# Scaling by 1 / std in the dealt output stages: from VectorE to GpSimd

## The chip, the core and the metric

The kernel runs on one core of a Trainium2 chip. The metric is the device time of one launch in microseconds (us). Everything is float32. Of the core's engines four compute here: TensorE (PE in the profile, with its weight loads as PEld), VectorE (DVE), ScalarE (ACT) and GpSimd (POOL). SyncE (SP) issues most of the DMAs. Each engine works through its own instruction stream in program order and waits for the others by semaphores.

## The reference

Two layers follow one another on x of shape (8, 64, 64, 192): `x = x + L(gn(x))`. Each L is a selective-scan block with 384 inner channels and 16 states; the first has 2 scan directions, the second 4. Cut to what matters here:

```python
xz = in_proj(gn(x)); xx, z = split(xz)
xc = silu(depthwise_conv3x3(xx))
for each direction:                    # 2 in the first layer, 4 in the second
    delta, Bs, Cs = projections of xc in that direction's order
    h = exp(delta * A) * h + (delta * xc) * B    # over 4096 positions
    y += sum over states of h * C                # plus xc * D
y = (y - mean(y)) * rsqrt(var(y) + 1e-5) * w + b # over the 384 channels
y = y * act(z)                                   # gelu, then silu
out = x + y @ out_proj
```

The change concerns the last four lines, the output stage, and in it the factor `rsqrt(var(y) + 1e-5)`, here called 1 / std.

## The kernel before, in words

**Tiling.** The 4096 positions of an image are cut into 8 chunks of T = 512. Channels lie on the 128 partitions, in DT = 3 channel tiles. A layer first runs a front part (`front`: projection and convolution for all 8 images) and then `scans`, which the change touches. There the work is a list of steps: for each image, for each direction, for each of 8 chunks. That makes 128 steps in the first layer and 256 in the second.

**Slots.** A step has NSL = 24 slots: 8 pairs of states times 3 channel tiles. In each slot DVE scans two states (`scan`, L736, two `tensor_tensor_scan` of 512) and POOL multiplies the result by C (`hc`, L737, 128x1024). Before that, PE must have put the scan's input into PSUM (`inject`, `hb`, L695, 16 matmuls), two slots ahead with two buffers, and ACT must have made the decay factors (`decay`, `da`, L712, two activations), four slots ahead with five buffers. After it, PE sums the products of a group of three slots into `py` (`reduce`, `py`, matmuls recorded at L152), 24 matmuls for each of the group's two states; the two are emitted at slots 5 and 5 after the group's first in the first layer, at 5 and 6 in the second. `h` has two buffers, `hc` and the C rows `cr` three each, all by groups of three slots. So the first layer has 3072 slots and the second 6144.

**Order.** The order on each engine is written out by hand. Everything that is not one of the four regular operations is entered with `at(step, slot, function)` at a slot given in a table (`L0_SLOTS`, `L1_SLOTS`), and the loop at the end emits it:

```python
                if 0 <= g < N * NSL:
                    scan(i, s)
                for f, a in sorted(todo.pop(g, []), key=lambda fa: rank_of.get(fa[0], 1.5)):
                    f(*a)
                if 0 <= g + 2 < N * NSL:
                    inject(g + 2)
                if 0 <= g + 4 < N * NSL:
                    decay(g + 4)
```

So in a slot each engine gets the scan's part first, then the entered functions, then the injection for two slots on and the decay for four slots on. Slot numbers above 23 run on into the following steps. "Slot 72" of the second layer is thus slot 0 of the third step after the one in which an output stage begins.

**Dealt output stages.** While image b + 1 is scanned, the 8 output stages of image b are dealt out: one every 2 steps (48 slots) in the first layer, one every 4 steps (96 slots) in the second. With 7 images and 2 layers these are 112 dealt stages. The output stages of the last image (8 in each layer, tables `L0_LAST` and `L1_LAST`) have their own slots and are called "own stages" below; their scaling stays where it was. A dealt stage runs on tile `yc` of 128 x 3 x 512:

- mean by matmuls, kept through the one-buffer tile `sm` (L871), and subtracted on DVE (`f_center`, L878); the squares likewise, ending in `pm` in PSUM
- `f_rstd`: Ln (L885) and Exp with scale -0.5 (L886) on ACT, both in PSUM
- `f_scale`: one DVE multiplication of all three tiles by 1 / std out of PSUM (L889)
- `f_affine`: weight and bias, ACT, one instruction for each channel tile (L897)
- `f_times`: product with the gate, POOL, one for each channel tile (L906)
- `f_out`: the output projection, PE, 3 matmul pairs for each of two output halves (`po`, L912), and `f_add`, DVE (L921)

The small PSUM results (`pd`, `pt`, `pb`, `pq`, `pz`, `ps`, `pm`, `po`) share one buffer, tag "m": the next can be written only when the one before it has been read.

Near a dealt stage's scaling in the second layer, the slot tables also place the preparation of the next step: `x_proj` (`pd`, L560) at slots 73, 73 and 75, its copy `x_dbl` (L570, ACT) at 76, `dt_proj` (`pt`, L608) at 77, 80 and 82, and `keep_y` at slot 77: the ACT copy (L785) of the finished step's `py` out of PSUM. `py` has one buffer, so the first `reduce` of the running step, also emitted at slot 77, waits for that copy.

Of the kernel before, what the change touches and what calls it, by code (L numbers as in the profile page):

```python
# [8 lines left out]
F32 = mybir.dt.float32  # L9
AF = mybir.ActivationFunctionType  # L10
# [5 lines left out]
P = 128  # L16
# [8 lines left out]
DT = 3  # L25
NS = 16
T = 512
NCH = L // T
RB = T // W
Q = 32  # L30
# [38 lines left out]
    "f_center": 24,  # L69
    "f_square": 24,  # L70
    "f_rstd": 33,
    "f_scale": 33,
    "f_act": 34,
    "f_affine": (36, 35, 34),
    "f_times": (38, 39, 36),
    "f_out": ((42, 42, 42), (44, 46, 46)),
    "f_add": (43, 47),
}

L0_LAST = {  # L80
# [35 lines left out]
    "f_center": 48,  # L116
    "f_square": 48,
    "f_rstd": 72,
    "f_scale": 72,
    "f_act": 59,  # L120
    "f_affine": (72, 76, 72),
    "f_times": (76, 79, 72),
    "f_out": ((83, 84, 84), (89, 91, 94)),
    "f_add": (85, 95),
}
# [377 lines left out]
def scans(tc, name, x_src, x_dst, xcd, xcd_col, xtd, xdd, t, dirs, rank, row_b, gate, slots, last, consts, dram):  # L503
# [5 lines left out]
    nc = tc.nc  # L509
# [27 lines left out]
    with tc.tile_pool(name=f"{name}_s1", bufs=1) as s1, tc.tile_pool(  # L537
        name=f"{name}_s2", bufs=2
    ) as s2, tc.tile_pool(name=f"{name}_psy", bufs=1, space=PSUM) as psy, tc.tile_pool(
        name=f"{name}_psh", bufs=2, space=PSUM  # L540
# [4 lines left out]
        def at(i, s, f, *a):  # L545
            todo.setdefault(i * NSL + s, []).append((f, a))
# [248 lines left out]
        fin = {}  # L795
# [71 lines left out]
                )  # L867

        def f_keep_sum():
            fin["sm"] = s1.tile([DT * Q, T], F32, name="sm")  # L870
            nc.scalar.copy(fin["sm"], fin["ps"][: DT * Q])  # L871

        def f_all(key):
# [7 lines left out]
            fin["sq"] = s1.tile([P, DT, T], F32, name="y" if end else "xn_sq")  # L881
            nc.scalar.activation(fin["sq"], fin["y"], AF.Square)

        def f_rstd():
            nc.scalar.activation(fin["pv"], fin["pv"], AF.Ln, bias=eps_ln)  # L885
            nc.scalar.activation(fin["pv"], fin["pv"], AF.Exp, scale=-0.5)  # L886

        def f_scale():
            nc.vector.tensor_mul(  # L889
# [40 lines left out]
        def thrice(i, s, f, *a):  # L930
            for p, q in enumerate(s):
                at(i, q, f, *a, p)

        for i in range(N):
# [22 lines left out]
            b, k, cols, rev, ci, c = steps[i]  # L957
# [9 lines left out]
        e = 0  # L967
        for b in range(B - 1):
            for c in range(NCH):
                e = max(e + K, (b + 1) * K * NCH - NCH + c + 1)  # L970
                at(e, 0, f_load_x, b, c)
                at(e, 6, f_load, b, c)
                at(e, slots["f_norm"], f_norm, b, c)
                for dt in range(DT):
                    thrice(e, slots["f_gate"][dt], f_gate, dt)
                    at(e, slots["f_keep"][dt], f_keep, dt)
                for w, (src, key) in enumerate((("y", "pm"), ("sq", "pv"))):
                    at(e, slots["f_sum"][w], f_sum, src)
                    at(e, slots["f_keep_sum"][w], f_keep_sum)
                    at(e, slots["f_all"][w], f_all, key)  # L980
                for f in f_center, f_square, f_rstd, f_scale, f_act:
                    at(e, slots[f.__name__], f)
                for dt in range(DT):
                    at(e, slots["f_affine"][dt], f_affine, dt)
                    at(e, slots["f_times"][dt], f_times, dt)
                for u in range(CT):
                    thrice(e, slots["f_out"][u], f_out, u)
                    at(e, slots["f_add"][u], f_add, u)
                at(e, slots["f_add"][1], f_store, b, c)
        for c in range(NCH):  # L990
            b, e, own = B - 1, N - NCH + c + 1, last
            if c == NCH - 1:

                own, l = dict(last), last["load"]
                at(N - 1, 20, f_load_last, b, c)
                own["f_norm"], own["f_act"] = l, l + 4
                own["f_gate"] = [(l + d, l + d) for d in range(DT)]
                own["f_keep"] = [l + d + 1 for d in range(DT)]
                own["f_mean"] = [[l + 5] * DT, [l + 7] * DT]
                own["f_center"], own["f_square"], own["f_rstd"], own["f_scale"] = l + 6, l + 6, l + 8, l + 9  # L1000
                own["f_affine"], own["f_times"] = [l + 10, l + 10, l + 11], [l + 11, l + 11, l + 12]
                own["f_out"], own["f_add"] = [[l + 12, l + 12, l + 13], [l + 15] * DT], [l + 14, l + 16]
                at(e, l, f_load, b, c)
            else:
                at(e, own["load"], f_load_x, b, c)
                at(e, own["load"], f_load, b, c)
            at(e, own["f_norm"], f_norm, b, c)
            for dt in range(DT):
                thrice(e, own["f_gate"][dt], f_gate, dt)
                at(e, own["f_keep"][dt], f_keep, dt)  # L1010
            for w, (src, key) in enumerate((("y", "pm"), ("sq", "pv"))):
                thrice(e, own["f_mean"][w], f_mean, src, key)
            for f in f_center, f_square, f_rstd, f_scale, f_act:
                at(e, own[f.__name__], f, *((c == NCH - 1,) if f is f_square else ()))
            for dt in range(DT):
                at(e, own["f_affine"][dt], f_affine, dt)
                at(e, own["f_times"][dt], f_times, dt)
            for u in range(CT):
                thrice(e, own["f_out"][u], f_out, u)
                at(e, own["f_add"][u], f_add, u)  # L1020
            at(e, max(own["f_add"]), f_store, b, c)
# [29 lines left out]
def vss_layer(tc, name, x_src, x_dst, w, dirs, rank, row_b, gate, slots, last, consts, dram):  # L1051

    with ExitStack() as ctx:
        xcd, xcd_col, xtd, xdd, *dram = dram
        if any(cols for cols, rev in dirs):
            xdd = None
        else:
            xcd_col = None
        t = load_weights(tc, ctx, name, w, len(dirs), rank, row_b + 2 * NS, consts[1])
        clear = dram[-1] if xcd_col is None else ()  # L1060
        front(tc, name, x_src, xcd, xcd_col, xtd, xdd, w["in_proj"][:, :D], t, clear, consts)
        scans(tc, name, x_src, x_dst, xcd, xcd_col, xtd, xdd, t, dirs, rank, row_b, gate, slots, last, consts, dram)
# [99 lines left out]
```

## Time and profile before

| What | Value |
|---|---|
| time, median of 3 runs | 26029.92 us (26021.06 to 26032.92) |
| profiled execution, its own time | 26028.44 us |
| span of that execution, first to last instruction | 26026.6 us |
| granted TensorE clock, mean | 0.988 |
| scans of the first layer | from 1025 to 9136 us, 3072 slots, 2.64 us each |
| scans of the second layer | from 10337 to 25982 us, 6144 slots, 2.55 us each |
| POOL busy / instructions | 22104.7 us / 9615 |
| L737 on POOL | x9216, mean 2370 ns |
| L878 on DVE, the subtraction of the mean | x128, mean 1730 ns |
| L885 and L886 on ACT, Ln and Exp | x128 each, mean 654 and 582 ns |

A "busy" share counts the time in which an engine has an instruction under way. Idle time in a row stands just before the instruction, with the engine and line that ended it. A timeline row merges instructions of one group that follow each other: start, duration of the whole row, engine, line, output and inputs, count. Instructions of one engine overlap by some hundredths of a microsecond, so the distance between two starts is a little shorter than the mean duration.

### The profile page before, as it was taken

The numbers are of one execution on the slowest core, as the hardware profiler recorded it, in microseconds if no ns is written. First come the engines' busy times: TensorE is split into PE (matmuls) and PEld (weight loads), VectorE is DVE, ScalarE is ACT, GpSimd is POOL, SyncE is SP. The second block draws the span as 40 slices with busy tenths as digits, with TensorE's granted clock in tenths as the row PEclk, the third lists the DMA queues.
The fourth block names the chain that finished last, engine by engine and source line by source line (L and its number), as shares of the span: only waits on it lengthen the run. The fifth ranks groups of instructions, "written<-read, shape, count | busy, mean of one in ns | idle before, by whom it ended". The sixth has DMA issues, their size and how long they took to land.

```text
span 26026.6 us, 785972 instructions
## 1 busy us (share of the span) xinstructions
PE 24190.1 (93%) x340032; PEld 13575.8 (52%) x340032; DVE 24270.1 (93%) x22142; ACT 17787.7 (68%) x28084; POOL 22104.7 (85%) x9615
## 2 busy tenths in 40 slices
PE   8999999999999877999999999999999999999999
PEld 4455555555555533555555555555555555555554
DVE  7899999999999855999999999999999999999998
ACT  4567777777777655666767767767767767767766
POOL 0399999999999701999999999999999999999997
PEclk9999999999999988999999999999999999999999
DMA  4566666666666556576576576576576576576574
GB/s 153 145 154 158 153 154 154 155 158 155 156 155 154 136 149 159 163 161 166 164 164 166 164 163 166 163 163 166 163 164 167 163 163 167 164 163 167 164 163 140
DMA packets 4225339, 4140.59 MB, mean 159 GB/s; under 512 B 2532524, under 2 KB 2732868, under 8 KB 4221892
## 3 DMA queue, kind: packets, MB, share of 16 engines
q1 hardware_dynamic: 3819760, 4032.72, 60.1%
q10 hardware_dynamic: 402132, 57.59, 1.3%
q8 instruction: 2692, 44.11, 0.7%
q14 instruction: 755, 6.18, 0.1%
HBM read 3443.63 MB, written 645.99 MB: 157 GB/s over the span
## 4 chain that ended last, share of the span: by engine, by line
PE 40%; DVE 38%; ACT 10%; issue 9%; ACTq 1%; DMA 1%; POOL 0%; SPq 0%; DVEq 0%; POOLq 0%
DVE h L736 33%; PE hb L695 17%; PE py L152 11%; ACT da L712 3%; PE pt L608 2%; PE pz L835 2%; PE pd L560 2%; PE po L912 2%; DVE tp L353 2%; DVE dut L658 1%; ACT delta L145 1%; ACT L145 1%; PE pc L152 1%; ACT L632 1%; ACTq L384 1%
## 5 line engine op out<-in xcount | busy, mean ns | idle before, releaser
L737 POOL TENSOR_TENSOR hc<-h,cr 128x1024 f32<-128x1024 f32 x9216 | 21639.8, 2370 | 3773.7 <-DMA xt_k<-xtd 2178.2
L736 DVE TENSOR_TENSOR_SCAN h<-da,st,hb 128x512 f32<-128x512 f32 x16128 | 19187.5, 1258 | 629.8 <-PE hb L695 560.6
L712 ACT ACTIVATE da<-delta,a_neg 128x512 f32<-128x512 f32 x18432 | 12142.9, 713 | 3225.2 <-DVE h L736 3218.7
L695 PEld LDWEIGHTS hb<-dg,dut 64*128 64x128 f32 x147456 | 9260.3, 186 | 7083.1 <-issue 5877.6
L695 PE MATMUL hb<-dg,dut 64*128 64x128 f32 x147456 | 10909.6, 287 | 908.9 <-DVE h L736 639.5
L152 PE MATMUL py<-hc,mask 32*32 32x512 f32 x147456 | 6882.8, 603 | 0.2
L152 PEld LDWEIGHTS py<-hc,mask 32*32 32x32 f32 x147456 | 1571.9, 103 | 2348.3 <-issue 1770.6
L736 DVE TENSOR_TENSOR_SCAN h<-da,hb 128x512 f32<-128x512 f32 x2304 | 2611.8, 1199 | 135.1 <-PE hb L695 122.4
L742 ACT COPY st<-h 128x6 f32<-128x6 f32 x2688 | 532.9, 198 | 1844.2 <-DVE h L736 1843.7
L353 DVE SCALAR_TENSOR_TENSOR tp<-pad,cw,tp 128x512 f32<-128x512 f32 x1344 | 991.0, 750 | 592.3 <-ACT tp L347 537.8
L608 PE MATMUL pt<-xdbl,w_dt 96*128 96x512 f32 (+1 forms) x2304 | 1302.9, 647 | 49.5 <-DVE yc L878 34.9
L650 PE MATMUL pq<-ident,delta 128*128 128x128 f32 x4608 | 760.4, 288 | 387.7 <-DVE dut L658 333.7
L622 ACT ACTIVATE delta<-pt,dtb 128x512 f32<-128x512 f32 x1152 | 783.9, 681 | 485.4 <-PE pt L608 485.3
L835 PE MATMUL pz<-xn_sq,w_in 96*128 96x512 f32 x1536 | 826.1, 637 | 38.0 <-ACT xn_sq L823 14.8
L658 DVE TENSOR_TENSOR dut<-pq,xt_k 128x512 f32<-128x512 f32 x1152 | 765.8, 665 | 88.2 <-PE pq L650 88.2
L560 PE MATMUL pd<-x_k,w_x 128*128 128x512 f32 x1536 | 798.3, 629 | 30.9 <-DVE yc L878 15.1
L912 PE MATMUL po<-yc,w_out 128*96 128x512 f32 x1536 | 787.4, 624 | 16.8 <-POOL yc L906 15.0
L650 PEld LDWEIGHTS pq<-ident,delta 128*128 128x128 f32 x4608 | 485.2, 141 | 586.9 <-DVE dut L658 472.7
L321 PE MATMUL pi<-x,w_x 128*128 128x512 f32 x768 | 427.0, 664 | 313.7 <-ACT x L301 124.1
L906 POOL TENSOR_TENSOR yc<-yc,g 128x512 f32<-128x512 f32 x384 | 491.0, 1281 | 126.4 <-ACT yc L897 123.6
L152 PE MATMUL pc<-pad,taps 32*32 32x512 f32 x13824 | 575.9, 592 | 12.2 <-ACT xo L368 12.2
L145 ACT ACTIVATE delta<-delta 128x1536 f32<-128x1536 f32 x384 | 570.5, 1486 | 4.3
(105 smaller groups left out, 9921.3 us busy)
## 6 DMA issues: line engine op xcount, KB each, us to landing
cr<-cscr SPq DMA_DIRECT2D x2048, 512.0 KB
dg<-dgd SPq DMA_DIRECT2D x1536, 512.0 KB
cr<-xdd SPq DMA_DIRECT2D x1024, 512.0 KB
xt_k<-xtd SPq DMA_DIRECT2D x768, 384.0 KB
xcd<-xo SPq DMA_DIRECT2D x128, 768.0 KB
xtd<-xv SPq DMA_DIRECT2D x128, 768.0 KB
y<-yrow SPq DMA_DIRECT2D x128, 768.0 KB
yc<-yrow SPq DMA_DIRECT2D x128, 768.0 KB
```

Source lines behind the costliest of these rows:

```text
L145: nc.scalar.activation(out, in_, AF.Softplus)
L152: nc.tensor.matmul(out[j * Q : (j + 1) * Q, dt], w[i * Q : (i + 1) * Q], x[i * Q : (i + 1) * Q], start=first, stop=last, tile_position=(i ...
L353: nc.vector.scalar_tensor_tensor(tv, window(dt, c, s), cw[:, dt, s : s + 1], tv, ALU.mult, ALU.add)
L560: nc.tensor.matmul(live[i]["pd"][:R], w_x[:, dt, k, :], live[i]["x"][:, dt], start=(dt == 0), stop=(dt == DT - 1),)
L608: nc.tensor.matmul(pt, w_dt[:, k, dt * P : (dt + 1) * P], live[i]["xdbl"][:rank], start=True, stop=True,)
L650: nc.tensor.transpose(pq[:, g], live[i]["delta"][:, dt, g * P : (g + 1) * P], ident)
L695: nc.tensor.matmul(hv[:, r, q], live[i]["dut"][r * G : (r + 1) * G, dt, q], dg[r * G : (r + 1) * G, q, :, 2 * mm : 2 * mm + 2], start=True ...
L712: nc.scalar.activation(da[:, n].rearrange("p (r g j) -> p r g j", r=2, j=G), live[i]["delta"][:, dt].rearrange("p (g r j) -> p r g j", r=2 ...
L736: nc.vector.tensor_tensor_scan(o, a, v, init, ALU.mult, ALU.add)
L737: nc.gpsimd.tensor_mul(hc[:, dt], h[:, dt], live[i]["cr", m])
L835: nc.tensor.matmul(fin["pz"], w_in[:, u, dt * P : (dt + 1) * P], fin["xn"][:, u], start=(u == 0), stop=(u == CT - 1),)
L912: nc.tensor.matmul(fin["po"][:CP], w_out[:, dt, u * CP : (u + 1) * CP], fin["y"][:, dt], start=(dt == 0), stop=(dt == DT - 1),)
```

## The change

Three things are changed in `scans`:

- In the dealt stages 1 / std goes to SBUF: Exp writes a new tile of the one-buffer name `sm`, which is now declared with 128 rows instead of 96. In the own stages it stays in PSUM (`end=True`).
- In the dealt stages the one DVE multiplication of 128 x 1536 becomes three POOL multiplications of 128 x 512, one for each channel tile, each in a slot of its own (33, 34, 35 and 72, 73, 74), after that slot's product `hc`.
- Affine, gate product, and in the first layer some output projections and additions, get other slots.

```diff
 L0_SLOTS
-    "f_scale": 33,
+    "f_scale": (33, 34, 35),
     "f_act": 34,
-    "f_affine": (36, 35, 34),
-    "f_times": (38, 39, 36),
-    "f_out": ((42, 42, 42), (44, 46, 46)),
-    "f_add": (43, 47),
+    "f_affine": (35, 36, 37),
+    "f_times": (38, 39, 40),
+    "f_out": ((42, 42, 43), (45, 46, 46)),
+    "f_add": (44, 47),
...
 L1_SLOTS
-    "f_scale": 72,
+    "f_scale": (72, 73, 74),
     "f_act": 59,
-    "f_affine": (72, 76, 72),
-    "f_times": (76, 79, 72),
+    "f_affine": (74, 75, 76),
+    "f_times": (77, 78, 79),
...
         def f_keep_sum():
-            fin["sm"] = s1.tile([DT * Q, T], F32, name="sm")
+            fin["sm"] = s1.tile([P, T], F32, name="sm")[: DT * Q]
...
-        def f_rstd():
+        def f_rstd(end=False):
             nc.scalar.activation(fin["pv"], fin["pv"], AF.Ln, bias=eps_ln)
-            nc.scalar.activation(fin["pv"], fin["pv"], AF.Exp, scale=-0.5)
+            fin["rs"] = fin["pv"] if end else s1.tile([P, T], F32, name="sm")
+            nc.scalar.activation(fin["rs"], fin["pv"], AF.Exp, scale=-0.5)
+
+        def f_scale_one(dt):
+            nc.gpsimd.tensor_mul(fin["y"][:, dt], fin["y"][:, dt], fin["rs"])
...
-                for f in f_center, f_square, f_rstd, f_scale, f_act:
+                for f in f_center, f_square, f_rstd, f_act:
                     at(e, slots[f.__name__], f)
                 for dt in range(DT):
+                    at(e, slots["f_scale"][dt], f_scale_one, dt)
                     at(e, slots["f_affine"][dt], f_affine, dt)
```

The second layer's `f_out` and `f_add` keep their slots: (83, 84, 84), (89, 91, 94) and (85, 95).

More of the change, by code (lines that the diff above doesn't have):

```diff
@@ L1013, in scans @@
             for f in f_center, f_square, f_rstd, f_scale, f_act:
-                at(e, own[f.__name__], f, *((c == NCH - 1,) if f is f_square else ()))
+                at(e, own[f.__name__], f, *((c == NCH - 1,) if f is f_square else (True,) if f is f_rstd else ()))
             for dt in range(DT):
```

## The prediction

> **What bounds the kernel now.** I began with the busy shares and the windows of the two scan stretches.
>
> ```profile
> 1025.00:9136.00 8111.00, 7584.86 (x106602) 4473.34 (x106600) 7748.12 (x6776) 5732.71 (x9000) 7444.05 (x3261) 0.99 0.64 153
> 10337.00:25982.00 15645.00, 14782.01 (x212326) 8226.34 (x212332) 15181.61 (x13304) 10883.77 (x17306) 14649.13 (x6333) 1.00 0.63 164
> ```
>
> The columns are the stretch, its length, then busy time of PE, PEld, DVE, ACT and POOL. DVE is busy 96 and 97%, PE 94%, POOL 92 and 94%. Three engines are nearly full, so what ends last changes from slot to slot, and the average can't say what an edit is worth. It is read around slots 33 and 72. The groups give durations:
>
> ```profile
> L889 DVE TENSOR_TENSOR yc<-yc,pm 128x1536 f32<-128x1536 f32 x128 | 221.6, 1731 | 61.8 <-ACT pm L886 61.8
> L906 POOL TENSOR_TENSOR yc<-yc,g 128x512 f32<-128x512 f32 x384 | 491.0, 1281 | 126.4 <-ACT yc L897 123.6 <-ACT g L894 2.8
> L785 ACT COPY y<-py 128x1536 f32<-128x1536 f32 x384 | 547.5, 1426 | 21.2 <-PE py L152 21.2
> ```
>
> L889 is the operation removed, L906 the shape of those added, L785 the copy that will matter. Then the timeline of one dealt stage of the second layer, POOL first, slot 71 to slot 76:
>
> ```profile
> 19799.08 4.75 POOL L737 TENSOR_TENSOR hc<-h,cr 128x1024 f32<-128x1024 f32 x2
> 19804.51 1.28 POOL L906 TENSOR_TENSOR yc<-yc,g 128x512 f32<-128x512 f32 x1 [0.68 <-ACT yc L897]
> 19805.74 9.36 POOL L737 TENSOR_TENSOR hc<-h,cr 128x1024 f32<-128x1024 f32 x4
> 19815.04 1.31 POOL L906 TENSOR_TENSOR yc<-yc,g 128x512 f32<-128x512 f32 x1
> ```
>
> POOL has no gap but 0.68 us: from start to start an `hc` takes 9.30 / 4 = 2.33 us and a 128x512 product 1.23. ACT, same stage:
>
> ```profile
> 19799.72 0.58 ACT L886 ACTIVATE pm<-pm 128x512 f32<-128x512 f32 x1
> 19802.91 1.52 ACT L897 ACTIVATE yc<-yc,lnb,lnw 128x512 f32<-128x512 f32 x2 [2.61 <-DVE yc L889]
> ...
> 19810.49 0.81 ACT L897 ACTIVATE yc<-yc,lnb,lnw 128x512 f32<-128x512 f32 x1
> 19811.21 1.32 ACT L712 ACTIVATE da<-delta,a_neg 128x512 f32<-128x512 f32 x2
> 19812.44 1.42 ACT L785 COPY y<-py 128x1536 f32<-128x1536 f32 x1
> ```
>
> 1 / std is ready at 19800.3, and the copy of `py` ends at 19813.86. PE:
>
> ```profile
> 19813.54 1.13 PE L608 MATMUL pt<-xdbl,w_dt 96*128 96x512 f32 x2
> 19814.60 1.11 PE L152 MATMUL py<-hc,mask 32*32 32x512 f32 x24
> ...
> 19819.55 1.20 PE L695 MATMUL hb<-dg,dut 64*128 64x128 f32 x16 [0.19 <-DVE h L736]
> ...
> 19829.29 1.11 PE L152 MATMUL py<-hc,mask 32*32 32x512 f32 x24
> ```
>
> From 19812.4 until slot 87 (19838.3) PE shows one idle stretch, 0.19 us; in slots 77 to 86 DVE waits for its injections (0.35 and 1.03 us at slots 85 and 86). There PE is the bound, and a late `py` moves everything after it. In the first layer, at slot 33:
>
> ```profile
> 5418.67 2.13 PE L695 MATMUL hb<-dg,dut 64*128 64x128 f32 x32
> 5418.41 1.72 DVE L889 TENSOR_TENSOR yc<-yc,pm 128x1536 f32<-128x1536 f32 x1
> 5420.06 5.96 DVE L736 TENSOR_TENSOR_SCAN h<-da,st,hb 128x512 f32<-128x512 f32 x5
> ```
>
> The scan after L889 starts at 5420.06; the first of the two injections, which it needs, takes about 1.19 us and ends at 5419.86.
>
> [...]2370 - 1281 = 1089 ns for 512 more elements is 2.13 ns[...], against 1731 ns for 1536 on DVE. [...]the scans here read one input from PSUM, and L737 stays between 2335 and 2507 ns beside them, so I charge no contention. [...]the 2.61 us before L897 held up all of ACT.
>
> **The change, part by part.** Times are against the profiled execution (26028.4 us with a span of 26026.6); the median, 26029.9, is 1.5 higher, and I add the difference to it.
>
> *DVE loses L889.* 112 dealt stages x 1.65 us (19802.79 - 19801.15 and 5420.06 - 5418.41, start to start) = 185 us. In the first layer the cover is PE: without L889 the scan could start at 5419.98, since it starts 0.12 us after its injection's end when it waits for it. That is a gain of 0.08, and 0 in the quarter of the stages whose step starts a new sequence (scans are 2.22 instead of 2.34 us a slot there). In the second layer PE gets ahead: its waits of 0.36, 0.47, 0.10 and 0.27 us between slots 72 and 77 go, and `pd` no longer waits for L889 to free the shared PSUM buffer. What is late next is `py` at slot 77, so this gain is lost again.
>
> *POOL gains three products a stage,* 336 x 1.23 = 413 us of busy time: 3.7 us in slots 72 to 74, where no room was. The product does not appear in the trace before; L906 has its shape, with both inputs in SBUF. I take 1.23 us. [...]above, I allow 1.6, 0.3 more than L906.
>
> *ACT now waits for POOL.* `hc` of slot 72 ends at 19803.83. Then come a product, `hc` 73, a product, `hc` 74, a product: 3 x 1.23 + 2 x 2.33 = 8.35, so the third product ends at 19812.2. DVE delivers in time: scans 73 and 74 end near 19803.5 and 19805.9. The third affine (slot 76) waits for it on ACT; queued behind it are two decays and, at slot 77, the copy of `py`. From start to start these are 0.72 (19811.21 - 19810.49) and 1.23 (19812.44 - 19811.21), then 1.42 for the copy: it ends at 15.6 in place of 13.86, and `py` can start at 19815.65 in place of 14.60, 1.05 later. Less the 0.19 idle, 0.86 us stay. The decays are still early: those of slot 80 end near 19814.2, scan 80 needs them at 19.5.
>
> The same four times in each of the 56 dealt stages of the second layer fall into four kinds. 21 are like this one. 21 run at the start of a sequence, where `py` came at 0.5 us earlier: 1.55 us stay. In 14 PE was later anyhow: 7 give 0, 7 give 0.3. Sum: 21 x 0.86 + 21 x 1.55 + 7 x 0.3 = 53 us.
>
> *POOL's backlog.* `hc` of slot 80 comes 3 x 1.23 - 0.68 = 3.0 us later: 19826.86 (before) becomes 19829.9. PE's `py` on it starts at 19829.29, with the 0.86 at 19830.15. It fits by 0.2 us, in other kinds by 0.1; DVE's second `h` buffer asks the same at slot 84, where it is not last. I charge 0.1 us in half of the stages, 3 us. SP's `cr` loads follow `hc` by the same 3 us; they are issued some 12 us ahead, so they stay covered, and the loads of `y` and `dg` behind them have 8 slots or more. The gate products, moved to 77 to 79, are as many as before; the third ends near 19827.7, before PE's output projection at 19828.3.
>
> *First layer, later slots.* No copy of `py` is near. ACT's three table loads hold the affines until after 5426, later than POOL's first scale (5422.3); the third product ends at 5429.6, before the third affine's turn at about 5431. The third gate product ends at 5445.0, and PE reaches the moved matmul at 5445.3; `hc` 41 ends at 5447.3, PE reaches it at 5447.4. PE ends the stage when it did. DVE waits 0.40 and 0.45 us for injections at slots 44 and 46, which the moved projections advance; at slot 49 its scan starts 0.46 after its injection, so 0.34 at most is won: about 0.25 in 42 stages. In the 14 at the start of a sequence POOL's backlog makes PE about 0.4 late. -10 + 6 = -4 us.
>
> The f_rstd edit, the same instruction into SBUF: 0, as ACT has 0.6 us free behind it. Sum: 53 + 3 - 4 = +52 us: 26,080 for the profiled execution, 26,082 for the median.
>
> **The rivals.**
> - *POOL's backlog decides (slower).* If a scale takes 1.6 us in place of 1.28, the third product and `hc` 80 come 1.0 later, and both waits grow by it: 56 x 1.0 more, 26,138. It decides from a margin of 0.1 us. For it: POOL runs gapless from slot 73 to 85. Against it: L906 varies from 1256 to 1344 ns only.
> - *The DVE pause was on the path (faster).* DVE is the busiest engine, and 185 us come off it. With the 53 us still paid, 26,030 - 185 + 53 = 25,898. Against it: injections arrive only 0.2 us ahead at slot 34.
> - *The wait of ACT is absorbed (no change).* If PE had slack in slots 77 to 86 that the records don't show, only the first layer's -4 is left: 26,026. For it: matmul ends are modelled. Against it: DVE's waits at 85 and 86.
> - That the products don't go to POOL can't be: the program lists 336 of them there, one after each `hc`.
>
> **How the numbers follow.** A measurement of this kernel tells about 0.2% (52 us) from no change. My forecast has 0.62, with its own range 26,050 to 26,115, and straddles that line: 0.33 slower, 0.29 within. POOL's backlog 0.17, slower. Absorbed 0.14, within. The DVE pause 0.07, faster. Together: slower 0.50, within 0.43, faster 0.07. The range goes from the absorbed case to the backlog case, 26,022 to 26,138.
>
> **What would show it.** In the profile after: ACT waits on POOL for L902 (the affine), some 4 us a stage in the second layer; the `y` copy ends 1.7 us later, counted from slot 71; `py` directly behind it; DVE waits for PE by some 1.7 us more at slot 79. No new wait of PE on POOL over 0.2 us. I am wrong if second-layer stages keep their length (243 us a stage), if the first layer changes by over 20 us, or if POOL's products take over 1.4 us.

## The result and the profile after

The changed kernel took 26131.19 us (median of 6 runs, 26121.47 to 26151.78), the kernel before, beside it, 26024.96 us (6 runs). The ratio is 1.0043, 95% interval 1.0030 to 1.0056: slower by about 106 us, where 52 were forecast.

The profiled span grew from 26026.6 to 26127.8 us, by 101.2. The starts and ends of the scans split that: front of the first layer +2.2, its scans -32.9, between the layers -2.2, scans of the second layer +132.8, tail +1.3. The two stretches again (length, then busy time of PE, PEld, DVE, ACT, POOL):

```profile
1027.00:9102.00 8075.00, 7571.81 (x106591) 4452.86 (x106596) 7665.52 (x6720) 5739.73 (x9000) 7621.01 (x3428) 0.99 0.64 154
10305.00:26077.00 15772.00, 14832.85 (x212280) 8257.82 (x212278) 15098.35 (x13247) 10892.32 (x17304) 14833.42 (x6498) 0.99 0.62 162
```

DVE's busy time fell by 83 us in each stretch and POOL's rose by 177 and 184, less than the 97 and 214 us a layer that were moved, since the busy time of their other instructions shifted as well. The load went where the edit sends it; yet the second layer is longer. The groups of instructions:

```profile
L736 DVE TENSOR_TENSOR_SCAN h<-da,st,hb 128x512 f32<-128x512 f32 x16128 | 19199.4, 1259 | 788.4 <-PE hb L695 703.6 <-ACT da L712 42.6 <-POOL hc L737 3.1
L152 PE MATMUL py<-hc,mask 32*32 32x512 f32 x147456 | 6899.2, 603 | 126.2 <-ACT y L785 125.9 <-issue 0.2
L891 POOL TENSOR_TENSOR yc<-yc,sm 128x512 f32<-128x512 f32 x336 | 427.7, 1273 | 0.0
L902 ACT ACTIVATE yc<-yc,lnb,lnw 128x512 f32<-128x512 f32 x384 | 308.9, 809 | 289.9 <-POOL yc L891 269.5 <-DVE yc L894 20.4
```

The wait in the second row is new: PE stood 125.9 us before `py` for ACT's copy `y` (none before). ACT stood 269.5 us before the affines for POOL's products, 4.8 us in each dealt stage of the second layer. A stage of the timeline shows the chain, from slot 71 (19841.03) on. POOL, then ACT, then PE and DVE:

```profile
19848.35 1.26 POOL L891 TENSOR_TENSOR yc<-yc,sm 128x512 f32<-128x512 f32 x1
19849.57 2.37 POOL L737 TENSOR_TENSOR hc<-h,cr 128x1024 f32<-128x1024 f32 x1
19851.90 1.26 POOL L891 TENSOR_TENSOR yc<-yc,sm 128x512 f32<-128x512 f32 x1
19853.12 2.38 POOL L737 TENSOR_TENSOR hc<-h,cr 128x1024 f32<-128x1024 f32 x1
19855.46 1.27 POOL L891 TENSOR_TENSOR yc<-yc,sm 128x512 f32<-128x512 f32 x1
```

```profile
19856.76 0.81 ACT L902 ACTIVATE yc<-yc,lnb,lnw 128x512 f32<-128x512 f32 x1 [1.05 <-POOL yc L891]
19857.48 1.32 ACT L712 ACTIVATE da<-delta,a_neg 128x512 f32<-128x512 f32 x2
19858.71 1.42 ACT L785 COPY y<-py 128x1536 f32<-128x1536 f32 x1
```

```profile
19856.45 1.12 PE L608 MATMUL pt<-xdbl,w_dt 96*128 96x512 f32 x2
19860.27 1.99 PE L152 MATMUL py<-hc,mask 32*32 32x512 f32 x24 [2.70 <-ACT y L785]
19862.19 2.08 PE L695 MATMUL hb<-dg,dut 64*128 64x128 f32 x16
...
19864.74 1.88 PE L152 MATMUL py<-hc,mask 32*32 32x512 f32 x24
```

```profile
19864.39 2.45 DVE L736 TENSOR_TENSOR_SCAN h<-da,st,hb 128x512 f32<-128x512 f32 x2 [3.90 <-PE hb L695]
```

Counted from slot 71, the copy ends at 19.10 (forecast 19.15) and `py` starts at 19.24 (forecast 19.20). The wait is the one forecast. What the forecast lacks is in the second column: 24 `py` matmuls take 1.99 us instead of 1.11 and 16 `hb` matmuls 2.08 instead of 1.19. The windows of these stretches give the reason in the column after the engines, the granted clock:

```profile
19856.00:19860.00 4.00, 1.57 (x12) 0.61 (x8) 4.00 (x4) 3.24 (x4) 4.00 (x3) 0.94 0.44 141
19860.00:19863.40 3.40, 3.13 (x34) 1.50 (x36) 0.48 (x1) 3.40 (x8) 3.40 (x2) 0.50 0.58 182
```

In this stage PE's clock is halved 2.0 us after its last matmul ended, and PE, late already, does its next work at half speed. The clock records of the trace give the start and length of each such half-clock stretch. They begin at slot 78 in 33 of the 56 dealt stages of the second layer (in none before); 17 last 3.4 us and 16 last 6.8.

In 42 of the stages PE stands 2.7 to 3.1 us before `py`, in the other 14 at most 0.73. (Idle time is counted from the matmul ends of the profile, which are modelled.) The half clock came in 33 of the 42 and in none of the 14. It began 1.9 to 4.7 us after PE's last matmul had ended, in some stages after PE had begun to work again. What sets the 33 apart from the other 9 is not shown: PE stood 2.69 to 3.09 us in the ones, 2.77 to 3.01 in the others.

### The profile page after: what moved, and what is told of

Read it like the earlier page. It is cut to its first block, busy times and chain, and to the rows that moved or that the text cites. A ratio compares the mean times of both kernels' runs of the same rounds, so it can differ in the third digit from the quotient of the medians.

```text
span 26127.8 us, 786420 instructions
## 1 busy us (share of the span) xinstructions
PE 24241.1 (93%) x340032; PEld 13590.3 (52%) x340032; DVE 24105.7 (92%) x22030; ACT 17804.0 (68%) x28084; POOL 22474.7 (86%) x9951
## 4 chain that ended last, share of the span: by engine, by line
PE 42%; DVE 35%; issue 9%; ACT 9%; POOL 4%; DMA 1%; ACTq 1%; SPq 0%; DVEq 0%; POOLq 0%
DVE h L736 30%; PE hb L695 17%; PE py L152 12%; POOL hc L737 3%; ACT da L712 3%; PE pt L608 2%; PE po L917 2%; PE pz L835 2%; DVE tp L353 2%; PE pd L560 2%; DVE dut L658 1%; PE pc L152 1%; ACT delta L145 1%; ACTq L384 1%; ACT L145 1%
## 5 line engine op out<-in xcount | busy, mean ns | idle before, releaser
L736 DVE TENSOR_TENSOR_SCAN h<-da,st,hb 128x512 f32<-128x512 f32 x16128 | 19199.4, 1259 | 788.4 <-PE hb L695 703.6
L152 PE MATMUL py<-hc,mask 32*32 32x512 f32 x147456 | 6899.2, 603 | 126.2 <-ACT y L785 125.9
L736 DVE TENSOR_TENSOR_SCAN h<-da,hb 128x512 f32<-128x512 f32 x2304 | 2617.7, 1200 | 243.3 <-PE hb L695 227.7
L835 PE MATMUL pz<-xn_sq,w_in 96*128 96x512 f32 x1536 | 833.2, 642 | 38.5 <-ACT xn_sq L823 15.3
L917 PE MATMUL po<-yc,w_out 128*96 128x512 f32 x1536 | 802.1, 628 | 18.3 <-POOL yc L911 15.3
```

What stands on the lines that cost most here:

```text
L152: nc.tensor.matmul(out[j * Q : (j + 1) * Q, dt], w[i * Q : (i + 1) * Q], x[i * Q : (i + 1) * Q], start=first, stop=last, tile_position=(i ...
L736: nc.vector.tensor_tensor_scan(o, a, v, init, ALU.mult, ALU.add)
L835: nc.tensor.matmul(fin["pz"], w_in[:, u, dt * P : (dt + 1) * P], fin["xn"][:, u], start=(u == 0), stop=(u == CT - 1),)
L917: nc.tensor.matmul(fin["po"][:CP], w_out[:, dt, u * CP : (u + 1) * CP], fin["y"][:, dt], start=(dt == 0), stop=(dt == DT - 1),)
```

## The experiments

"Stage" is the time from one dealt stage's first scan to the next one's; before, its mean is 125.33 us in the first layer and 243.61 in the second. Each ratio is to the kernel before beside it (26007 to 26014 us), with its 95% interval. L1 in a diff is the second layer, L0 the first. Theory A of the first run is the prediction's wait of ACT with the half clock added.

**Third affine behind the copy.** In `L1_SLOTS`:

```diff
-    "f_affine": (74, 75, 76),
+    "f_affine": (74, 75, 77),
```

> The changed kernel, but in the second layer the third affine stands at slot 77, behind the copy of py, in place of 76. Theory A (the late copy of py costs about 1 us a stage, and TensorE's half clock after its idle stretch costs the rest of the 2.4 us): the copy now waits for the second product only, py at slot 77 can start 17.4 us after slot 71 in place of 19.2, no half-clock stretch is left at slot 78; then hc of slot 80, which ends 33.4 us after slot 71, is what PE waits for at slot 83 (it would be there at about 32.0), so the second layer's stages stay about 0.7 us longer than before and the time falls by some 95 us from 26,131 to 26,036. Theory B (POOL's backlog of hc makes all of the 2.4 us, the copy is a bystander): the backlog is the same, 26,131 stays.

Measured: 26052.57 us, 1.0016 (1.0008 to 1.0024). The stage falls from 246.00 to 244.40 us, and no half-clock stretch is left at slot 78, as Theory A had it. The time is 39 us over the kernel before in place of 106, where it hoped for 11. Slot 83 is 1.33 us longer than before, and it is not PE that waits there, as expected (11.7 us for `hc` in the whole trace), but DVE, at the scan of slot 84 (61.1 us for `hc` in the whole trace). DVE, then POOL ahead of it:

```profile
20086.81 4.65 DVE L736 TENSOR_TENSOR_SCAN h<-da,hb 128x512 f32<-128x512 f32 x4 [1.75 <-POOL hc L737]
```

```profile
20079.62 1.27 POOL L911 TENSOR_TENSOR yc<-yc,g 128x512 f32<-128x512 f32 x1
20080.86 2.36 POOL L737 TENSOR_TENSOR hc<-h,cr 128x1024 f32<-128x1024 f32 x1
20083.18 1.26 POOL L911 TENSOR_TENSOR yc<-yc,g 128x512 f32<-128x512 f32 x1
20084.41 6.99 POOL L737 TENSOR_TENSOR hc<-h,cr 128x1024 f32<-128x1024 f32 x3
```

Scan 84 overwrites the `h` that `hc` 80 reads (the first of the last three), and all three gate products stand ahead of that, two of them in these lines. In the changed kernel itself this wait is nearly hidden (5.3 us over both kinds of scan, 2.3 before), because DVE is late by then anyhow. Take one wait away and the next one shows.

**First layer alone.** `L1_SLOTS` and the second layer's stages as before; the first layer as changed.

```diff
-    "f_scale": (72, 73, 74),
+    "f_scale": 72,
-    "f_affine": (74, 75, 76),
-    "f_times": (77, 78, 79),
+    "f_affine": (72, 76, 72),
+    "f_times": (76, 79, 72),
```

> First layer as in the changed kernel, second layer's slots and DVE scaling as before. If the layers add up as the two traces show (first -33 us, second +133 us), the time is 26,025 - 33 = 25,992, and the second layer's stages keep 243.5 us. If the first layer's gain was an accident of where TensorE's half-clock stretches fall in one execution, it is 26,025.

Measured: 25999.77 us, 0.9996 (0.9988 to 1.0004), stages 124.92 and 243.55 us. The first layer's part can't be told from nothing; the loss is the second layer's.

**Filling the stretch without work.** The changed kernel, but `dt_proj` of slot 77 is done twice more in the second layer, for nothing, so that PE works while it waits for the copy:

```diff
+                if xdd is None:
+                    at(e, 77, dt_again, e + 4)
```

> The changed kernel, but in the second layer's 56 stages PE repeats the projection of slot 77 twice into the same tile (two times 1.05 us) in the stretch in which it waits for the copy of py. Theory A: half-clock stretches at slot 78 fall from 33 to under 8, a stage keeps only the copy's own delay of about 1 us in place of 2.4, so the time falls by about 70 us to 26,060. Theory B (the clock plays no part): the matmuls fit into idle time, 26,131 stays; and if PE had not been idle there, 56 x 2.1 = 118 us come on top.

Measured: 26085.66 us, 1.0027 (1.0017 to 1.0038). Half-clock stretches at slot 78: none in place of 33; stage 245.07 us. PE's wait for the copy in the second layer:

```profile
PE py L152 <- ACT y L792: 44.0, 42, 1.4
```

These are 44.0 us in 42 waits, the longest 1.4, in place of 125.9. PE does more work, and the kernel is 34 us closer to the one before (72 us over it in place of 106); Theory A hoped for more, 26,060. The second-layer scans fall by 51 us in the profiles, though the added work costs about 1 us in each of the 14 stages that had no long wait. So the clock takes over 50 us of the 132.8.

**Slots alone.** All of the changed kernel's later slots, with the scaling on DVE out of PSUM as before:

```diff
-    "f_scale": (33, 34, 35),
+    "f_scale": 33,
...
-    "f_scale": (72, 73, 74),
+    "f_scale": 72,
```

> All slots of the changed kernel, but the scaling is back on DVE, in one instruction at slots 33 and 72, with 1 / std in PSUM. Theory C (the first layer's 33 us come from the moved projections and additions): the first layer keeps its gain, 30 to 35 us, the second has no wait of ACT on POOL and is within 10 us of before: 25,990. Theory D (they come from DVE being relieved): the first layer is as before, 26,025.

Measured: 26040.58 us, 1.0012 (1.0004 to 1.0021); stages 125.47 and 243.67 us. The second layer doesn't mind the later slots, so its loss needs POOL's products. The first layer gets no gain from them: Theory C falls. It is 0.14 us a stage longer than before, with 13 half-clock stretches at slot 35 in place of 6.

**Half the filling.** As the filling above, with one repetition:

```diff
-            for _ in range(2):
+            for _ in range(1):
```

> The changed kernel, but dt_proj of slot 77 is repeated once (not twice) in the second layer: TensorE's stretch of 2.7 to 3.0 us without work before py becomes one of about 1.1 us of work and 1.6 to 1.9 us without. No result of the computation changes. Theory A[...]: 0 to 10 stretches at slot 78 in place of 33, and the time is within 10 us of the run with two repeats, 40 us below the changed kernel. Theory B[...]: 20 or more stretches remain, time near that of the changed kernel, ratio 1.0035 or more.

Measured: 26115.51 us, 1.0045 (1.0031 to 1.0059), no better than the changed kernel. 32 half-clock stretches remain at slot 78. PE's waits:

```profile
PE py L152 <- ACT y L792: 80.3, 42, 2.3
```

80.3 us in 42 stages are 1.9 us each. Theory A's forecast fails and B's comes true. With two repetitions the same row was 1.0 us in each stage, up to 1.4, and no stretch was left: the second repetition makes the difference.

**Gate products behind `hc` 80.** The third affine as in the first run, and:

```diff
-    "f_times": (77, 78, 79),
-    "f_out": ((83, 84, 84), (89, 91, 94)),
-    "f_add": (85, 95),
+    "f_times": (80, 81, 82),
+    "f_out": ((88, 89, 89), (91, 92, 94)),
+    "f_add": (90, 95),
```

> The second layer's third affine stays one slot later (77, behind the copy of py), and its gate products go from slots 77, 78, 79 to 80, 81, 82, behind the hc of slot 80; the output projections follow (88, 89, 89 and 91, 92, 94; the sums at 90 and 95). Everything else is as in the changed kernel. With only the affine moved, slot 83 was 1.33 us longer, by DVE's scan 84 waiting for POOL. Theory A (hc 80 is late because the gate products stand ahead of it): slot 83 goes back to within 0.3 us of the kernel before, the sum over slots 72 to 87 falls from +0.7 to between -0.3 and +0.2 us a stage, and the time is some 40 us below that of the kernel with the affine alone moved: a ratio of 0.999 to 1.001. Theory B (3.7 us of products a stage are more than POOL can take at all, wherever they stand): the wait turns up at another hc, the stage stays 0.7 us longer than before, ratio 1.0012 to 1.002. Theory C (the output projections, pressed together behind slot 88, delay TensorE's injections): slots 88 to 92 get longer by over 0.5 us in all.

Measured: 26054.66 us, 1.0017 (1.0010 to 1.0023), stage 244.68 us: no gain on the first run. Slot 83 is as before, but DVE now waits for POOL at scan 87, three slots on, for the `hc` 83 that stands behind all three products:

```profile
20100.89 2.33 DVE L736 TENSOR_TENSOR_SCAN h<-da,hb 128x512 f32<-128x512 f32 x2 [1.49 <-POOL hc L737]
```

And slots 90 and 93 are 1.75 and 0.66 us longer, where the injections come late behind the projections; slot 85, which the projections left, is 1.77 shorter. B and C both hold, A's hope for the time doesn't. "Wherever they stand", as B has it, is refuted by the next run.

**Two gate products behind `hc` 80.** The third affine as in the first run, the projections in their slots:

```diff
-    "f_times": (77, 78, 79),
+    "f_times": (77, 80, 80),
```

> The second layer's third affine at slot 77 (behind the copy of py), and only the second and third gate products behind the hc of slot 80 (slots 77, 80, 80); the output projections keep the slots of the changed kernel (83, 84, 84 and 89, 91, 94). Theory A (two waits on GpSimd make the loss, of ScalarE for the third scale product and of VectorE for the hc of slot 80, and TensorE takes them over only because the projections were pressed together in the last run): both waits are gone and no new one comes, slot 83 and slots 85 to 90 are within 0.2 us of before, the second-layer stage is 243.5 to 243.8 us, and the time is 0.9990 to 1.0004 of before. Theory B (GpSimd has no room for 3.7 us more in any order): a new wait on an hc after slot 81 appears, stage 244.2 us or more, ratio 1.001 to 1.002. Theory C (the remaining loss is TensorE's own, in slots 76 to 79): slots 76, 78 and 79 keep their +0.41, +0.43 and +0.28, and since VectorE's 1.65 at slot 72 only pays for these, the stage ends near 243.5, which A also gives; a loss would then have to show in slots 85 to 90.

Measured: 26008.22 us, 1.0000 (0.9992 to 1.0008), stage 243.81 us. Slots 83 and 85 to 90 are as before, and DVE's waits for POOL are 5.9 us in the L736 row. With only three entries of the slot table moved, the loss of time is gone: ACT's wait for the third product, DVE's for `hc` 80, and what followed from them, were the loss. (ACT still waits 215 us in all for the first two products.) Slots 76, 78 and 79 keep their +0.42, +0.43 and +0.28, as Theory C had it, and the 1.65 us that DVE saves at slot 72 pay for them: in slots 66 to 90 the stages are 16 us shorter in all than before. What the mean stage keeps, 0.20 us, comes from slot 1, 0.39 us longer, of which the next run tells more.

**Scales ahead of `hc` 73.** As the last, and:

```diff
-    "f_scale": (72, 73, 74),
+    "f_scale": (72, 72, 73),
```

> As the kernel with two gate products behind the hc of slot 80, and besides the second scale product is issued at slot 72 and the third at 73, so that two stand ahead of the hc of slot 73. Theory A (the wait of ScalarE is for GpSimd's order): ScalarE's waits on GpSimd for the second and third affine fall from 1.4 and 1.0 us to under 0.3 us, slot 76 loses its +0.4 us since the copy of xdbl is no longer held up, and the stage is 0.2 to 0.5 us shorter than in the run beside it: 0.999 to 1.000 of before. Theory B (hc of slots 72 to 74, now up to 2.5 us later, are wanted by TensorE or VectorE): a wait on POOL of 0.5 us or more appears between slots 74 and 78, and the stage is no shorter or longer.

Measured: 26001.49 us, 0.9996 (0.9988 to 1.0004), stage 243.55 us. ACT's wait for the second product is gone, as A had it, but slot 76 keeps its +0.42. In slots 66 to 90 a stage is 0.75 us shorter than before (42 us in all). But slot 1 is 0.52 us longer on the mean, nearly all of it in every eighth stage, where it takes 5.3 to 8.9 us in place of 3.0 to 3.7. PE there, then SP's last loads ahead of it:

```profile
22976.59 2.22 PE L152 MATMUL py<-y,mask 32*32 32x512 f32 x16
22981.86 2.04 PE L152 MATMUL py<-y,mask 32*32 32x512 f32 x8 [3.05 <-DMA y<-ycol]
22983.82 2.08 PE L695 MATMUL hb<-dg,dut 64*128 64x128 f32 x16
```

```profile
22975.38 2.12 SPq L681 DMA_DIRECT2D cr<-cscr  x1
22977.55 0.43 SPq L769 DMA_DIRECT2D y<-ycol  x1
```

The last part of `y` is issued 48.5 us after slot 78 of the stage before, in the kernel before 43.7 (in all seven such stages 45.6 to 48.5 against 42.3 to 44.4). In SP's queue it stands behind `cr` loads that wait for an `hc`. That the later `hc` make it late is argued from this order; adding `y` to `py` later would tell, and wasn't tried. Here, too, the clock is at half: the `hb` take 2.08 us.

**First layer, old projections.** The scaling of the first layer on POOL, its projections in their old slots, the second layer as before:

```diff
-    "f_out": ((42, 42, 43), (45, 46, 46)),
-    "f_add": (44, 47),
+    "f_out": ((42, 42, 42), (44, 46, 46)),
+    "f_add": (43, 47),
```

> Only the first layer has the scaling on GpSimd, and its output projections and sums stand in the slots of the kernel before (42, 42, 42 and 44, 46, 46; sums at 43 and 47); the second layer is that of the kernel before. In the stages without a half-clock stretch the first layer of the changed kernel was 0.5 us longer than before (slot 0 +0.74, slots 43 to 45 -0.57), and still its 56 stages were 22 us shorter on the mean of four profiles. Theory A (the slots of the projections cost the 0.5, and at the same time take away the 15 half-clock stretches at slot 2, which is worth more): slot 0 and slots 43 to 45 go back to the times of before, the stretches at slot 2 come back (10 or more), and the 56 stages are as long as in the kernel before, 125.2 to 125.5 us. Theory B (the gain is DVE's relief or the moved affines): the stages stay at 124.6 to 125.0 us whatever the clock does at slot 2. Theory C (the 0.5 us is POOL's backlog, not the projections): slot 0 stays 0.7 us longer.

Measured: 26055.08 us, 1.0016 (1.0010 to 1.0023), stages 125.89 and 243.59 us. Slot 0 goes back to its old time and 17 half-clock stretches come back at slot 2, as A had it; but slot 43 is 1.01 us longer, which no theory had:

```profile
PE po L917 <- POOL yc L911: 58.6, 55, 6.7
```

In the changed kernel this row has 15.3 us in 5 waits. The third gate product, at slot 40, reaches PE too late for slot 42; the change's later projections cover that.

## Why the prediction was right or wrong

*The forecast had the sign and, within 0.05 us in the stage shown, the wait of ACT; it missed that the stretch without work which it made was followed, in 33 of 56 stages, by half clock on PE.* The time, 26131, lies above its own range, 26,050 to 26,115. It is inside the wider one only because that reached to 26,138 for the case in which POOL's backlog decides, which is not what happened: that is luck. Term by term:

- **ACT's wait, second layer: 53 us forecast, 66 measured, and 62 on top from the clock.** Take slots 66 to 90, which lost 127.8 us over the 56 stages. In the 21 stages forecast at 0.86 all have the half clock; without it, in the run with the filling, they cost 1.20. In the 21 forecast at 1.55, the 9 at full clock cost 1.70. In the last 14, forecast at 0 and 0.3, it is 0.26 and 0.45. 21 x 1.20 + 21 x 1.70 + 7 x 0.26 + 7 x 0.45 = 66 us. The rest is the clock: the first 21 took 3.16 on the mean, 21 x (3.16 - 1.20) = 41; of the second, 12 took 3.42, 12 x (3.42 - 1.70) = 21. The step that failed is "`py` can start at 19815.65 in place of 14.60, 1.05 later": the delay was right, but `py` and what follows were priced at the durations of a PE that had not stood still. The forecast had both parts of the gap. PE is done with `dt_proj` 1.6 us earlier, counted from slot 71, since DVE's pause is gone ("PE gets ahead"), and `py` comes 1.1 us later; it never added them to a stretch of 2.7 us. The trace before had half-clock stretches too, 60 in the first layer's scans, and the forecast gave them no price. DVE's extra wait at slot 79, forecast at 1.7, was 3.90 in the stage shown, and 2.69 in the next one, at full clock.
- **POOL's backlog: 3 us forecast; DVE's waits for `hc` rose by 3.0, from 2.3 to 5.3,** and were not decisive. Without the half clock, in the run with the filling, they are 6.8, so the margin of 0.1 to 0.2 us was real. But it holds only while `py` is late: with ACT's wait for the third product gone, in the first run, they are 61.1 us, and slot 83 is 1.33 us longer. The rival that put 56 us on it had the right place but not the price: products took 1.253 to 1.305 us.
- **SP's loads "stay covered":** so they did in the changed kernel, where everything after the wait is late. In the two runs that remove the waits they are the likely next bound.
- **DVE's 185 us:** off the path in the changed kernel, as forecast. In the first layer the scan of slot 34 starts 0.13 us after its injection in place of 0.20:

```profile
5389.77 7.14 DVE L736 TENSOR_TENSOR_SCAN h<-da,st,hb 128x512 f32<-128x512 f32 x6 [1.49 <-PE hb L695]
```

  The rival that counted this gain is refuted.
- **POOL's products:** 336 x 1.273 = 428 us busy; the 1.23 from start to start holds. Why 1 / std moves to SBUF for them is not shown: no run has POOL read it out of PSUM.
- **First layer: -4 forecast; -32.9 in the profile, beyond the 20 us that I had named as wrong.** Eight profiles with this first layer have 8071.0 to 8095.9 us for its scans, mean 8084, against 8106.8 in the one profile before; in time, the run with the first layer alone gave 0.9996, -10 us with an interval of -31 to +10. In stages without a half-clock stretch it is not faster but 0.4 to 0.6 us slower (slot 0 +0.74, slots 43 to 45 -0.57), where I had -0.07: the moved projections press on slot 0. The gain goes with the clock: 43 half-clock stretches in 55 stages before, 15 of them at slot 2; 9 to 26 in the eight profiles, 0 or 1 at slot 2. In the time the two nearly cancel.
- **"Absorbed":** refuted; the wait came through in 42 of the second layer's 56 stages.

**What stays open.** Ahead of slot 35 PE stood in all 56 first-layer stages, 1.5 to 1.9 us before and 1.6 to 1.7 in the changed kernel; half clock began there in 6 of them before, 13 in the run with the slots alone, 0 to 5 elsewhere. Open, too, are the stretches at slots 2, 25 and 26 of the first layer (15, 4 and 12 before). At slot 2 a gap of 0.87 us went with 15, one of 0.54 with 0 or 1; idle time alone doesn't explain them.

## What to carry to other kernels

Work moved onto a nearly full engine, here GpSimd at 94%, delays what stands behind it in its queue, and the delay comes out where another engine's queue holds something urgent behind a wait for it: here a PSUM copy on ScalarE that ended 1.7 us later, behind an operation that itself was in no hurry. Price a stall of TensorE by its length and by the half-speed work that may come after it, here 66 and 62 us, and look for that in the durations of the next matmuls. A stall can be made of two parts that look harmless one by one: here TensorE came 1.6 us early and its input 1.1 us late. When a wait is removed and time returns only in part, compare slot by slot: here ScalarE's, VectorE's and TensorE's waits lay one behind the other, and moving three entries of a table cleared them, while freeing the busiest engine by 185 us shortened no run by more than its noise.

## What the runs showed of the hardware

- In the changed kernel TensorE's clock was halved (0.50 granted; in the stage shown 24 `py` matmuls took 1.99 us in place of 1.11) in 33 of the 42 stages in which it had stood 2.7 to 3.1 us, and in none of the 14 in which it had stood at most 0.73.
- Two needless matmul pairs that fill the gap remove that part of the loss: 33 stretches became none, and 51 us of the second layer's scans went away. One pair, leaving 1.9 us, changed next to nothing (32 stretches).
- GpSimd's 128x512 product took 1.253 to 1.305 us in all 336 cases beside a VectorE at 92%. A slowdown that fell on all of them alike could not be seen here.
